# Cross-attention on one core: batch 0's fifth key chunk, the tokens' values and maxima, and the warm-up products

## The chip, the cores and the metric

The kernel runs on one core of one Trainium2 chip. The metric is the device time in microseconds of one execution, the lower the better; runs of the kernel before and after are compared. The engines are named as in the profile: PE (TensorE, matmuls, with PEld for its weight loads), DVE (VectorE), ACT (ScalarE), POOL (GpSimd) and SP (SyncE, which issues most of the DMAs). All data is float32.

## The reference

There are 16 batches of 100 queries, 640 wide, 8 heads of 80. Each batch has 722 context rows of width 384; the last 4 of them are the "tokens", the first 718 the keys.

```python
query = hidden_states @ Wq                      # 100 x 640
keyt, valt = enc @ Wk, enc @ Wv                 # 718 x 640 each
hs = _mha(query, keyt, valt)                    # main attention
ca_q1 = einsum('btc,th->bch', ca, Wq_ca)[:, indices]
ca_hs1 = _mha(ca_q1, residual, residual)        # tokens' first attention (100 x 100)
ca_hs2 = _mha(ca_hs1 @ Wq, ca @ Wk_ca, ca @ Wv_ca)  # tokens' second (100 x 4)
out = (hs + ca_hs2) @ Wout + b_out + residual
```

`_mha` is softmax attention by heads, scaled by 80 ** -0.5.

## The kernel before

The work goes batch by batch, and each batch's iteration also prepares the next ones. In iteration b the kernel makes, for batch b, the scores in three groups (`scores`, L785), the running maximum over the keys (`larger`, L1495; class `Maximum`, L875), the subtraction and exponential of the three score tiles `st` (L1484, L1492), the values (class `Values`, L426) and the attention product `a_ps` (L1741); for batch b + 1 the keys (class `Keys`, L469) and the tokens' first attention (class `Second`, L949); for batch b + 2 the loads.

**Products in forms.** Keys and values are made by a scheme with 15 products of sums ("forms") in place of 18. The sums of the context are made by POOL (`enc_sums`, L497), 13 operations a batch; the sums of the weights once at the start (`weight_sums`, L524), on DVE and POOL. A product is accumulated in a PSUM bank, and after each product the bank is read: copied by ACT the first time a target is written, added by DVE afterwards (`Blocks.go`, L412). So a bank must be read before the next product adds to it. The keys have five chunks of 128 columns; four of them come from `Keys`, the fifth from class `Chunk` (L730): 16 products of 64 columns, two side by side, put between the attention products of the batch before at the places `steps` (L1714 to L1717). For batch 0 itself, the fifth chunk comes from `last_keys` (L720): nine products of 128 columns by 240 keys straight from the raw context, into the two banks of a `pair`, and two ACT copies.

**Tokens.** `Second.products` makes y, DVE takes the part g from it (`take`, L980), POOL multiplies and adds four times for the scores e (`scores1`, L989: L997, L1004), DVE makes their maximum (`softmax1`, L1009) and ACT the exponential (`exponentials1`, L1027). The maximum runs in steps: a transpose, quad, side, mx, spread, a transpose to over, then the subtraction. With `scalar` two spread copies go to ACT, without it one goes to DVE and mx takes four reductions in place of two. The flag `fine` cuts the steps smaller, and `go(n)` lets n of them pass, so the calls with numbers decide where each step stands on its engine. The tokens' values `va` are made once for all batches (L1427 to L1444): six matmuls, an ACT copy, two DMAs to DRAM. Their weights `wvca` stand in one of the two `enc` buffers, into which batch 1's context is loaded later (`load_enc`, L230).

**Kinds of batches.** `PAIRS` names the batches after which two blocks of 128 output rows are projected at once (`project_pair`, L1248); this happens in iterations 3, 6, 8, 11 and 13. `MIXED` are the odd iterations 3 to 13, in which the next pair's queries are made. `PLAIN` (L41) are those without either: 0, 2, 4, 10, 12 and 14.

**Order.** Before the batch loop a planner orders each engine's instructions by their readiness in its model; `tc.issue_after` and `keep_in_program_order` add constraints on one engine. From the loop on (`tc.manual_schedule`, L1462) every engine takes its instructions in the order of the program. The planner may still put early instructions of the loop among the last ones ahead of it. PE, DVE, ACT, POOL and SP's queue each work in order.

PSUM has three pools of two: `pair` (two banks at once), `psumk` and `psum1`; `psum` alternates between the last two. The `wide` tiles of the maxima have two buffers.

Of the kernel before, what the change touches and what calls it, by code (L numbers as in the profile page):

```python
# [40 lines left out]
PLAIN = [b for b in range(B - 1) if b not in (1, *MIXED) and b - 1 not in PAIRS]  # L41
# [101 lines left out]
def kernel(  # L143
# [260 lines left out]
    class Blocks:  # L404
# [7 lines left out]
        def go(self, n=1):  # L412
            for _, (k, (bank, f, to)) in zip(range(n), self.plan):
                first = bank not in self.opened
                if first:
                    self.opened[bank] = self.open(bank)
                at = self.opened[bank]
                self.product(at, f, first, self.ends[bank] == k)
                for out, left in self.places(at, to):
                    if to in self.begun:  # L420
                        self.moved = nc.vector.tensor_tensor(out, left, out, ALU.add)  # L421
                    else:
                        self.moved = nc.scalar.copy(out, left)  # L423
                self.begun.add(to)
# [450 lines left out]
    class Maximum:  # L875
# [12 lines left out]
        def steps(self, top):  # L888
# [24 lines left out]
            if not (self.fine and scalar) or self.fine == "plain":  # L913
                yield
# [34 lines left out]
    class Second:  # L949
# [14 lines left out]
        def products(self):  # L964
# [14 lines left out]
            self.y_v = y_ps[:S, : NH * HG].rearrange("p (h k) -> p h k", h=NH)  # L979
        def take(self, lo, hi):  # L980
            return nc.vector.tensor_copy(self.g[:, lo:hi], self.y_v[:, lo:hi, :T])

        def copy(self):
            self.y = y_sbs[self.b % 2]
            nc.scalar.copy(self.y[:, :, :HT], self.y_v[:, :, T:])
            if self.b > 0:
                self.take(0, NH)
# [21 lines left out]
        def softmax1(self, n=9, hold=False):  # L1009

            if not self.top:
                after = self.b - 1
                self.top = Maximum(
                    e1,
                    f"1_{self.b}",
                    after - 1 in PAIRS or after in PLAIN,
                    "plain" if after in PLAIN else after in MIXED or after - 1 in PAIRS,
                )
# [8 lines left out]
        def exponentials1(self):  # L1027
            nc.scalar.activation(e1[:S], e1[:S], AF.Exp, scale=SCALE)
# [97 lines left out]
    class Last:  # L1126
# [121 lines left out]
        def project_pair(self, between):  # L1248
# [41 lines left out]
            between(2 if self.b + 1 in MIXED else 3)  # L1290
# [4 lines left out]
            read(b4, 1, 0)  # L1295
            product(b2, [(two[:, 4:], last(1))], True)
            read(b2, 1, 1)
            product(b1, [(one[:, 2:4], w(1, 1)), (one[:, 4:], last(1))], False)
            read(b1, 0, 1)
            product(b3, [(two[:, :2], wout2[:, 0])], True)  # L1300
# [33 lines left out]
    for _ in range(5):  # L1334
        nc.tensor.matmul(idle_ps[:, :P], idle, idle, start=True, stop=True)
# [84 lines left out]
    with tc.issue_after(made.ins):  # L1420
        weight_sums(nc.gpsimd, wk4)
    with tc.issue_after(masked.ins):
        keys(load_m(1))
    last_keys(0, enc)
    Keys(0, enc).go(NF)

    va = wide("va")[:, : H // 2]  # L1427
    va_ps = psum("va_ps")
# [11 lines left out]
    for n in range(2):  # L1440
# [3 lines left out]
        )  # L1444
    with tc.issue_after(copied.ins):
# [17 lines left out]
    for b in range(B):  # L1463
# [52 lines left out]
        if b - 1 in PLAIN:  # L1516
            now.exponentials1()
# [12 lines left out]
        if b == 0:  # L1530
# [22 lines left out]
            less = subtract(2)  # L1553
            enc_next = load_rest(b + 2, enc_next)
            keys(m_next)
            now.values2(less)
            enc_sums(enc_next)
        elif b + 1 < B:
# [77 lines left out]
            if last.b in PAIRS:  # L1636
                last.project_pair(second.softmax1)
# [7 lines left out]
            if not mixed and b not in PLAIN:  # L1645
# [54 lines left out]
        if b < B - 1 and not b in MIXED:  # L1700
# [17 lines left out]
        for g in range(2):  # L1718
# [5 lines left out]
            for n, (h, i) in enumerate(order):  # L1724
                if b in PLAIN and (g, n) in ((1, 1), (1, 8), (1, 12)):
                    second.softmax1(1)
                if b < B - 1 and (g, n) in steps:
                    chunk.go()
                    if b not in MIXED and (g, n) == steps[-1]:
# [10 lines left out]
                for lo, hi in QC:  # L1740
# [7 lines left out]
                    )  # L1748
            if b in PLAIN and g == 0:
# [92 lines left out]
```

## Time and profile before

| | |
|---|---|
| three runs | 914.9, 914.14, 911.94 us |
| their median | 914.14 us |
| the profiled execution | 916.26 us |
| its span from first to last instruction | 914.5 us |
| PE busy | 902.7 us (99%) |
| DVE busy | 720.0 us (79%) |
| POOL busy | 706.4 us (77%) |
| ACT busy | 461.9 us (51%) |
| TensorE clock granted | 1.0 |

The profile's times count from the first instruction of the span. In the span the loop's first scores begin at 59.3 us, and those of batch 1 at 101.3 us. A row of a timeline has start, duration (both in us), engine, line of the kernel, operation, the tiles written and read, shapes, how many were merged, and in brackets the idle time before it and what ended it. Each float32 matmul appears as two records.

### The profile page before, as it was taken

How to read it: one execution, taken by the hardware profiler on the slowest of the kernel's cores; microseconds unless marked ns; L12 is line 12 of the kernel's file. 1: busy time of each engine (PE TensorE's matmuls, PEld its weight loads, DVE VectorE, ACT ScalarE, POOL GpSimd, SP SyncE). 2: the span in 40 equal slices, each digit the busy share in tenths (PEclk: the TensorE clock that was granted, in tenths of full speed). 3: DMA queues.
4: the chain of work that ended last, by engine and by line, in shares of the span. 5: the costliest groups of instructions: out<-in, count | busy, mean ns of one | idle time of the engine just before them, and what ended most of it. 6: DMA issues, size and time to landing. Idle time of an engine off the chain costs nothing.

```text
span 914.5 us, 28436 instructions
## 1 busy us (share of the span) xinstructions
PE 902.7 (99%) x12172; PEld 746.1 (82%) x12172; DVE 720.0 (79%) x1288; ACT 461.9 (51%) x907; POOL 706.4 (77%) x684
## 2 busy tenths in 40 slices
PE   9998999999999999999999999999999999999998
PEld 6886879888797878878788787988879888797866
DVE  2659896889848898796987869878895889848983
ACT  2334533747437473653736436364742747437441
POOL 7587999687967879697796968968797687976623
PEclk9999999999999999999999999999999999999999
DMA  8832002031300302131021301203120031310111
GB/s 257 268 96 79 30 32 85 24 106 53 96 18 27 104 24 83 54 86 51 33 75 54 105 32 47 61 25 106 54 81 32 25 106 54 91 37 24 61 46 38
DMA packets 50586, 62.99 MB, mean 69 GB/s; under 512 B 13682, under 2 KB 37810, under 8 KB 50460
## 3 DMA queue, kind: packets, MB, share of 16 engines
q1 hardware_dynamic: 48812, 59.18, 21.1%
q8 instruction: 96, 1.57, 0.7%
q10 hardware_dynamic: 1024, 1.15, 0.4%
q0 software_dynamic: 624, 0.85, 0.3%
q14 instruction: 30, 0.25, 0.1%
HBM read 55.59 MB, written 5.57 MB: 67 GB/s over the span
## 4 chain that ended last, share of the span: by engine, by line
PE 90%; DVE 4%; DMA 3%; SPq 1%; issue 0%; ACT 0%; ACTq 0%; DVEq 0%
PE s_ps L800 12%; PE a_ps L1741 11%; PE v_psA L450 11%; PE v_psB L450 9%; PE k_psA L481 8%; PE k_psB L481 7%; PE o_ps L1265 4%; PE k_psA L761 4%; PE v_psC L450 4%; PE k_psC L481 3%; PE q_ps L618 2%; PE q_ps L560 2%; PE v_psD L450 2%; PE v_psE L450 2%; PE q_psA L618 1%; DMA xT<-in_xt 1%
## 5 line engine op out<-in xcount | busy, mean ns | idle before, releaser
L997 POOL TENSOR_TENSOR e<-ca,g 100x800 f32<-100x800 f32 x64 | 98.0, 1542 | 100.2 <-ACT kT L423 76.2
L1741 PEld LDWEIGHTS a_ps<-vs,st 120*64 120x64 f32 (+3 forms) x3072 | 120.2, 124 | 10.5 <-issue 0.4
L1741 PE MATMUL a_ps<-vs,st 120*64 120x81 f32 (+3 forms) x3072 | 124.2, 233 | 0.0
L516 POOL TENSOR_TENSOR enc<-enc 128x240 f32<-128x240 f32 x144 | 111.7, 786 | 13.8 <-DMA enc<-in_enct 6.8
L1485 DVE TENSOR_TENSOR st<-st,over 120x1600 f32<-120x1600 f32 x48 | 115.2, 2401 | 0.0
L450 PE MATMUL v_psA<-wv_sb,enc 128*120 128x320 f32 x352 | 109.3, 433 | 0.0
L1112 POOL TENSOR_TENSOR hs<-hs,hs 100x640 f32<-100x640 f32 x48 | 94.8, 1975 | 3.8
L481 PE MATMUL k_psA<-enc,wk_sb 128*128 128x240 f32 x384 | 95.4, 371 | 2.1 <-DVE kT L421 1.7
L1105 POOL TENSOR_TENSOR hs<-vb,p 100x640 f32<-100x640 f32 x64 | 89.6, 1411 | 9.1 <-issue 4.8
L1004 POOL TENSOR_TENSOR e<-e,e 100x800 f32<-100x800 f32 x48 | 92.5, 1927 | 3.8
L450 PE MATMUL v_psB<-wv_sb,enc 128*120 128x320 f32 x296 | 91.8, 433 | 0.0
L481 PEld LDWEIGHTS k_psA<-enc,wk_sb 128*128 128x128 f32 x384 | 71.4, 190 | 18.6 <-POOL e L997 2.1
L450 PEld LDWEIGHTS v_psA<-wv_sb,enc 128*120 128x120 f32 x352 | 64.2, 183 | 25.0 <-DVE vs L421 0.5
L1493 ACT ACTIVATE st<-st 120x1600 f32<-120x1600 f32 x48 | 73.9, 1539 | 20.3 <-DVE st L1485 19.6
L1497 DVE TENSOR_TENSOR most<-most,st 120x800 f32<-120x800 f32 x64 | 68.3, 1068 | 14.2 <-ACT st L850 12.9
L481 PE MATMUL k_psB<-enc,wk_sb 128*128 128x240 f32 x320 | 78.0, 366 | 0.3 <-DVE sm L1087 0.3
L800 PE MATMUL s_ps<-qp,kT 64*64 64x100 f32 (+1 forms) x3072 | 73.4, 248 | 0.0
L450 PEld LDWEIGHTS v_psB<-wv_sb,enc 128*120 128x120 f32 x296 | 54.1, 183 | 21.9 <-DVE vs L421 0.4
L800 PEld LDWEIGHTS s_ps<-qp,kT 64*64 64x64 f32 (+1 forms) x3072 | 67.0, 130 | 5.6 <-issue 4.2
L1180 ACT COPY hsT<-turned_hs 32x160 f32<-32x160 f32 (+7 forms) x244 | 67.7, 278 | 3.0
L481 PEld LDWEIGHTS k_psB<-enc,wk_sb 128*128 128x128 f32 x320 | 60.6, 190 | 8.7 <-issue 0.7
L856 ACT COPY st<-s_ps 120x800 f32<-120x800 f32 x64 | 49.8, 830 | 34.3 <-PE s_ps L800 33.6
(209 smaller groups left out, 1904.2 us busy)
## 6 DMA issues: line engine op xcount, KB each, us to landing
vb<-va_d SPq DMA_DIRECT2D x62, 250.0 KB
enc<-in_enct SPq DMA_DIRECT2D x30, 240.0 KB
enc<-in_enct SPq DMA_DIRECT2D x15, 360.0 KB
xT<-in_xt SPq DMA_DIRECT2D x8, 500.0 KB
rest<-in_enct SPq DMA_DIRECT2D x31, 120.0 KB
xn<-in_x SPq DMA_DIRECT2D x11, 320.0 KB
out<-xn SPq DMA_DIRECT2D x11, 320.0 KB
ca<-in_cas SPq DMA_DIRECT2D x16, 156.2 KB
```

The source lines that it names most:

```text
L450: nc.tensor.matmul(at[0][j][:KN, : H // 2], a_form(self.enc, f)[:, j * KN : (j + 1) * KN], wv_there.get(f, wv_sb[:, W_AT[f]]), start=first ...
L481: nc.tensor.matmul(at[:, i * KT : (i + 1) * KT], wk_sb[:, W_AT[f], i], a_form(self.enc, f), start=(first and i == 0), stop=last, skip_grou ...
L516: nc.gpsimd.tensor_tensor(out, left, right, op)
L800: nc.tensor.matmul(s_ps[at][k0:k1, cols], w, rhs, start=not begun & {(at, k) for k in range(k0, k1, 32)}, stop=last, skip_group_check=True,)
L997: first = nc.gpsimd.tensor_tensor(to, self.ca[:, t, :].unsqueeze(1).to_broadcast([S, NH, S]), g[:, :, t].unsqueeze(2).to_broadcast([S, NH, ...
L1004: made = nc.gpsimd.tensor_tensor(e, e, to, ALU.add)
L1105: first = nc.gpsimd.tensor_tensor(to, self.vb[t][:S].rearrange("p (h d) -> p h d", h=NH), p2[:, :, t].unsqueeze(2).to_broadcast([S, NH, D] ...
L1112: nc.gpsimd.tensor_tensor(sums, sums, to, ALU.add)
L1485: return nc.vector.tensor_tensor(st[i], st[i], top.over[:KN].unsqueeze(1).to_broadcast([KN, 2, ROWS]), ALU.subtract,)
L1493: nc.scalar.activation(st[i], st[i], AF.Exp, scale=SCALE)
L1497: most_now = nc.vector.tensor_tensor(most[:KN], most[:KN], st[i][:, u], ALU.max)
L1741: nc.tensor.matmul(a_v[lo:hi, h % 4], st[i // 2][: KEYS[i], i % 2, h * S + lo : h * S + hi], block(i, h // 4)[: KEYS[i], h % 4], start=(i ...
```

## The change

`PLAIN` loses batch 0. Around that:

- **Warm-up.** 21 matmuls of 32 columns by 32 in place of 5 of 128 by 128.
- **Before the loop.** Batch 0's keys are made in two goes, eight products and seven; between them stand the tokens' values `va`, now in a bank of a `pair`. Batch 0's first maximum of the tokens (`softmax1`) moves from the loop's head to behind the last key addition, and the copy of `low` into the score tile's unused rows to behind the tokens' scores in the program.
- **Batch 0's iteration.** Batch 1's fifth key chunk is made by `last_keys` behind batch 0's keys, ahead of the attention, in place of `Chunk` inside it. The exponential of the third score tile comes right behind its subtraction. Batch 1's tokens' maximum runs on DVE alone: four steps behind batch 0's tail work, and the rest with the subtraction and the exponential behind the attention's second half, ahead of that half's normalisation.
- **Iterations 6 and 8.** The maximum's steps inside `project_pair` go 1, 2, 2, 1 in place of 1, 3, and the remaining ones behind it; over is made inside, and the subtraction moves into the attention's second half, at (1, 6).
- **Plain iterations (2, 4, 10, 12, 14).** The empty step ahead of spread is gone, so spread stands at the attention's place (1, 18), ahead of y's copy; the following batch makes the exponential of e in two halves.
- For batch 1, `take` stands ahead of y's copy in the program.

```diff
-PLAIN = [b for b in range(B - 1) if b not in (1, *MIXED) and b - 1 not in PAIRS]
+PLAIN = [b for b in range(2, B - 1) if b not in MIXED and b - 1 not in PAIRS]
...
-            if not (self.fine and scalar) or self.fine == "plain":
+            if not (self.fine and scalar):
                 yield
...
+            if b == 1:
+                self.take(0, NH)
...
-            if self.b > 0:
+            if self.b > 1:
                 self.take(0, NH)
...
-                    "plain" if after in PLAIN else after in MIXED or after - 1 in PAIRS,
+                    after in (*MIXED, *PLAIN) or after - 1 in PAIRS,
...
-        def exponentials1(self):
-            nc.scalar.activation(e1[:S], e1[:S], AF.Exp, scale=SCALE)
+        def exponentials1(self, parts=1):
+            w = ROWS // parts
+            for lo in range(0, ROWS, w):
+                part = e1[:S, lo : lo + w]
+                nc.scalar.activation(part, part, AF.Exp, scale=SCALE)
...
-            between(2 if self.b + 1 in MIXED else 3)
+            between(2)
             product(b4, [(two[:, 2:4], wout2[:, 1])], True)
             product(b1, [(sum1, w(0, 1))], False)
             read(b1, 1, 1)
             product(b4, [(two[:, 4:], last(0))], False)
             read(b4, 1, 0)
+            if self.b + 1 not in MIXED:
+                between(2)
             product(b2, [(two[:, 4:], last(1))], True)
             read(b2, 1, 1)
             product(b1, [(one[:, 2:4], w(1, 1)), (one[:, 4:], last(1))], False)
             read(b1, 0, 1)
+            if self.b + 1 not in MIXED:
+                between(1)
...
-    for _ in range(5):
-        nc.tensor.matmul(idle_ps[:, :P], idle, idle, start=True, stop=True)
+    for _ in range(21):
+        nc.tensor.matmul(
+            idle_ps[:32, :32], idle[:, :32], idle[:, :32], start=True, stop=True
+        )
...
     with tc.issue_after(made.ins):
         weight_sums(nc.gpsimd, wk4)
+        nc.scalar.copy(
+            sts[0].rearrange("p a r -> p (a r)")[96:],
+            low[96:].to_broadcast([P - 96, 2 * ROWS]),
+        )
...
-    Keys(0, enc).go(NF)
-
+    first_keys = Keys(0, enc)
+    first_keys.go(8)
     va = wide("va")[:, : H // 2]
-    va_ps = psum("va_ps")
+    va_ps = bank("va_ps")
+    turn[0] += 1
...
+    first_keys.go(NF)
+    with tc.issue_after(first_keys.added.ins):
+        second.softmax1()
...
-            now.softmax1()
-            nc.scalar.copy(
-                sts[0].rearrange("p a r -> p (a r)")[96:],
-                low[96:].to_broadcast([P - 96, 2 * ROWS]),
-            )
...
         if b - 1 in PLAIN:
-            now.exponentials1()
+            now.exponentials1(2)
...
             less = subtract(2)
+            exponential(2)
+            last_keys(b + 1, enc)
             enc_next = load_rest(b + 2, enc_next)
             keys(m_next)
             now.values2(less)
             enc_sums(enc_next)
+            second.softmax1(4)
...
-                last.project_pair(second.softmax1)
+                last.project_pair(lambda n: second.softmax1(n, True))
...
-            if not mixed and b not in PLAIN:
+            if b == 1:
                 second.softmax1(8)
...
-        if b < B - 1 and not b in MIXED:
+        if 0 < b < B - 1 and b not in MIXED:
             chunk = Chunk(b + 1, enc)
             chunk.go(2)
...
-                if b < B - 1 and (g, n) in steps:
+                if 0 < b < B - 1 and (g, n) in steps:
                     chunk.go()
+                    if b - 1 in PAIRS and b not in MIXED and (g, n) == (1, 6):
+                        second.softmax1()
...
+            if b == 0 and g == 1:
+                second.softmax1()
+                second.exponentials1()
```

More of the change, by code (lines that the diff above doesn't have):

```diff
@@ L420, in go @@
                     if to in self.begun:
-                        self.moved = nc.vector.tensor_tensor(out, left, out, ALU.add)
+                        self.added = nc.vector.tensor_tensor(out, left, out, ALU.add)
                     else:
-                        self.moved = nc.scalar.copy(out, left)
+                        nc.scalar.copy(out, left)
                 self.begun.add(to)
```

## The prediction

> **What bounds the kernel now.** First the page's totals, then the waits of TensorE (PE), since an engine that is busy all the time can only be helped by removing its work or its few gaps.
>
> ```profile
> span 914.5 us, 28436 instructions
> PE 902.7 (99%) x12172; PEld 746.1 (82%) x12172; DVE 720.0 (79%) x1288; ACT 461.9 (51%) x907; POOL 706.4 (77%) x684
> ```
>
> ```profile
> PE k_psA L481 <- DVE kT L421: 1.7, 1, 1.7
> ...
> PE w_ps L1394 <- DMA kT<-in_wkt: 1.1, 1, 1.1
> PE k_psA L761 <- DVE kT L751: 0.9, 2, 0.5
> PE k_psA L761 <- DVE kT L421: 0.9, 1, 0.9
> PE o_ps L1265 <- DVE xn L1276: 0.7, 2, 0.3
> PE m_ps L1370 <- issue: 0.5, 1, 0.5
> PE k_psA L481 <- DVE wk_sb L546: 0.5, 1, 0.5
> PE k_psB L481 <- DVE sm L1087: 0.3, 1, 0.3
> ```
>
> PE is idle for 914.5 - 902.7 = 11.8 us in all. A row gives the wait, what ended it, its sum, how often and the longest. With the 1.1 at the very start (the 1.13 row under Warm-up) they name 7.7 us; most of the rest is the end, when the last output leaves. So the change moves the time only where it touches one of these rows or alters what PE computes. By place: 3.2 us before 38 us (DVE's zeroing, weights that are late), 2.9 us in batch 0 (L421 twice, L1087), 1.6 us in two later batches (L751, L1276). Nothing stands for batches 1, 2, 4, 10, 12 and 14. Every forecast below is a subtraction from these rows, plus the difference in PE work.
>
> **Batches 6 and 8: the tokens' maximum.** These are the two batches that project a pair of row blocks, but make no queries. The timelines of PE and DVE in batch 6 show both waits; batch 8 has the same two (the rows above count two of each, 0.7 and 0.9 in all).
>
> ```profile
> 413.55 1.85 PE L1265 MATMUL o_ps<-wout_sb,hsT 128*128 128x320 f32 x6 [0.34 <-DVE xn L1276]
> ...
> 420.22 0.63 PE L761 MATMUL k_psA<-enc,w_sums 128*64 128x240 f32 x4 [0.45 <-DVE kT L751]
> ```
>
> ```profile
> 410.49 0.98 DVE L893 TENSOR_REDUCE quad<-turned 128x25 f32<-128x800 f32 x1
> 411.50 0.71 DVE L896 TENSOR_REDUCE side<-quad 32x25 f32<-32x25 f32 x4
> 412.24 0.65 DVE L905 TENSOR_REDUCE mx<-side 32x25 f32<-32x100 f32 x2
> 412.92 1.28 DVE L1276 TENSOR_TENSOR xn<-o_ps,xn 128x320 f32<-128x320 f32 x3
> ...
> 417.33 1.00 DVE L926 STREAM_TRANSPOSE over<-spread 128x800 f32<-128x800 f32 x1
> 418.36 1.36 DVE L1023 TENSOR_TENSOR e<-e,over 100x800 f32<-100x800 f32 x1
> ```
>
> PE's 0.34 waits for a bank that DVE reads at 412.92, because three steps of the maximum stand in front. The change lets two steps through there and puts mx behind the next read: the bank's read starts at 412.24, 0.65 earlier, more than 0.34. PE's 0.45 waits for the chunk's first additions, which DVE begins only when over (1.00) and the subtraction (1.36) are done, at 419.7. The change puts over ahead of the pair's last two reads and the subtraction into the second half of the attention, (1, 6). The additions start some 1.4 earlier, the subtraction's time, more than 0.45. What is late next: the two moved reads end about 1.0 later, but free a bank pair that the next scores alone take, some 10 us on; the subtraction runs among the attention's last 3 us, and only e's exponential, which ACT takes after it, needs it. I cost the new waits at nothing. Term: 2 x (0.34 + 0.45) = **-1.6 us**.
>
> **Batch 0's fifth chunk.** Before, 16 products of half width (two column halves side by side) run inside batch 0's attention; after, 9 full ones stand in front of it.
>
> ```profile
> 89.14 0.43 PE L761 MATMUL k_psC<-enc,w_sums 128*64 128x120 f32 x4
> 90.42 0.63 PE L761 MATMUL k_psA<-enc,w_sums 128*64 128x240 f32 x4 [0.85 <-DVE kT L421]
> ...
> 100.45 0.92 PE L970 MATMUL y_ps<-m,xT 128*64 128x72 f32 x20
> ```
>
> From the chain of waits, records of the same form as a full product, and of the attention:
>
> ```profile
> 38.27 0.81 PE k_psB L481 x4
> ...
> 97.68 1.69 PE a_ps L1741 x48
> ```
>
> ```profile
> 92.30 1.53 ACT L1493 ACTIVATE st<-st 120x1600 f32<-120x1600 f32 x1
> ```
>
> A full product of 240 columns is two records of 0.81 / 4 = 0.2025, so nine take 18 x 0.2025 = 3.65. Attention: 1.69 / 48 = 0.0352 a record, 192 of them 6.76. After: 3.65 + 6.76 = 10.41. Before: 89.14 to 100.45 is 11.31, the 0.85 wait in it. What they replace took 11.31 - 0.85 - 6.76 = 3.7, so PE's work stays the same and the wait goes: the full products go into a bank pair that no key product uses, and cover the time in which DVE empties k_psC. Term: **-0.9 us**; if the wait came back in front of them, it would be 0. ACT now makes st's last exponential before their two copies; it ends at 93.8, and the attention needs it at 89.1 + 3.65 and two thirds of its first half (2.25), 95.0. DVE loses seven additions of 0.41.
>
> **What DVE does in that room.**
>
> ```profile
> 90.28 1.81 DVE L1485 TENSOR_TENSOR st<-st,over 120x1600 f32<-120x1600 f32 x1
> ```
>
> Batch 1's maximum is now made by DVE alone (two more mx reductions, its own spread). Its over and subtraction stand ahead of the second half's normalisation, which frees a_ps. The last subtraction of st ends at 92.1. By batch 6's rows the transpose takes 1.0, quad 1.0, side 0.7, four mx 1.3 and spread, as wide as over, 1.0; over 1.0 and the subtraction 1.4 follow, and I add 0.7 for each half's normalisation: 100.9, and 100.0 with the shift of the next part. PE wants those banks in its second scores, near 101. I cost it at 0; the bound is the subtraction held up by two POOL products as long as L997's below, +3.0.
>
> **The tokens' values among the keys.** Rows of PE, SP, POOL and DVE, in this order:
>
> ```profile
> 48.84 1.83 PE L1431 MATMUL va_ps<-wvca,tokens 128*64 128x320 f32 x12
> 78.52 1.05 PE L481 MATMUL k_psA<-enc,wk_sb 128*128 128x240 f32 x4 [1.66 <-DVE kT L421]
> ```
>
> ```profile
> 50.72 1.82 SPq L234 DMA_DIRECT2D enc<-in_enct  x3
> ```
>
> ```profile
> 57.15 0.69 POOL L516 TENSOR_TENSOR enc<-enc 128x240 f32<-128x240 f32 x1 [3.02 <-DMA enc<-in_enct]
> ...
> 70.29 3.04 POOL L997 TENSOR_TENSOR e<-ca,g 100x800 f32<-100x800 f32 x2
> ```
>
> ```profile
> 63.37 1.02 DVE L1514 TENSOR_TENSOR most<-st 128x800 f32<-128x800 f32 x1 [4.68 <-ACT st L856]
> 65.70 2.93 DVE L1497 TENSOR_TENSOR most<-most,st 120x800 f32<-120x800 f32 x2 [1.31 <-ACT st L850]
> ...
> 69.13 0.18 DVE L981 COPY g<-y_ps 100x32 f32<-100x32 f32 x1
> 69.22 4.97 DVE L1497 TENSOR_TENSOR most<-most,st 120x800 f32<-120x800 f32 x2
> ```
>
> Batch 1's context goes into the buffer that the tokens' value weights hold, so its load (50.72) waits for the last va product. Seven of the fifteen key products, 0.81 each, now follow va: it ends 5.7 earlier, and POOL's sums can start up to 3.02 earlier, at 54.1. What follows on POOL shifts with them, but L997 needs g, which DVE makes at 69.13. DVE's maxima are the long pole: one takes 1.02 alone, yet the pair at 65.70 takes 2.93 beside POOL's sums, and the pair at 69.22 takes 4.97, the second one stuck until both L997 are through. PE waits 1.66 at 78.52 for what stands behind. With the sums over by 65, the first pair takes 2.0 and the rest of DVE's row starts 0.9 earlier; the second pair again meets L997, which I leave at 4.97, the row's own value. Term: **-0.9 us**, out of the 1.66. Bounds: -2.5, if it meets one L997 only; +1.0, if each of its two maxima waits in turn, for both L997 (3.0) and for the addition behind them (1.9, as long as L1004's mean on the page): 1.0 + 3.0 + 1.0 + 1.9 = 6.9 in place of 4.97, less the 0.9. The second maximum starts at about 70.2, before L997 at 70.29, and still ends after both: starting first did not give it its turn. The page "SBUF — State Buffer" of the Trainium skill ("Who interferes with whom") has whichever of the two issues first hold the shared port for its whole instruction, which this row doesn't bear out; by it the term would be -2.4, as in the third rival.
>
> The moved va brings its copy and two DMA issues to ACT among the key copies. They have the time of the three products after which a key bank is needed again, 2.4 us, and I cost them at 0; if they are longer, each us is lost once. The first tokens' maximum keeps its place on DVE, behind the last key addition and POOL's scores; batch 0's low copy was already early on ACT. Both 0.
>
> **Warm-up.** 21 small products replace 5; both end about where the first weights land.
>
> ```profile
> 1.13 2.50 PE L1335 MATMUL idle_ps<-idle 128*128 128x128 f32 x10 [1.13 <-DVE idle L1332]
> 3.62 1.42 PE L391 MATMUL v_ps<-wv_sb,rest 128*120 128x320 f32 x2
> ...
> 7.31 0.70 PE L391 MATMUL v_ps<-wv_sb,rest 128*120 128x320 f32 x2
> 7.85 1.24 PE L391 MATMUL v_ps<-wv_sb,enc 128*120 128x320 f32 x4
> ```
>
> Six value records take 3.7 us until 7.31, against 0.27 each after it (two in 7.31 to 7.85); the granted clock stands at 1.00 all the while, so only these durations show the slow start. Up to 2.1 could be won, or as much lost by a later switch, but PE afterwards waits 0.5 (L1370), 1.1 (L1394, a DMA) and 0.5 (L546, behind the wq loads): a gain ends in these waits, and a loss of up to 2.1 is covered by them. Term: 0.
>
> **Plain batches (2, 4, 10, 12, 14).** Spread moves ahead of y's copy on ACT, and the exponential of e is split in halves. PE waits for neither now; the split adds one instruction to ACT, at 51% the idlest engine. Term 0; uncovered, five times at most what the shortest copy in this list costs, 5 x 0.2 = +1.0.
>
> **Sum.** -1.6 - 0.9 - 0.9 = -3.4. The profiled execution took 916.26 (914.5 and 1.8 around it), 2.1 above the median of the three runs; the terms are differences, so I take them from the median: 914.14 - 3.4 = **910.8 us**.
>
> **Rivals.**
> - The load isn't earlier, because SP's queue or PE's order holds it back: SP's queue is served in order, and other loads wait in it; against it, its visible release is va's last product. Third term 0: -2.5, 911.7. Chance 0.18.
> - POOL's scores block each maximum in turn: third term +1.0, -1.5, 912.7. The 4.97 speaks for it; that DVE has its first maximum under way when g is out speaks against. Chance 0.14.
> - The port goes to the first starter: the second pair takes 1.0 + 1.5 + 1.0 = 3.5 in place of 4.97, -4.9 in all, 909.2. The start at 70.2 speaks against it. This is what "SBUF — State Buffer" of the Trainium skill would give. Chance 0.10.
> - A wait takes the removed one's place: a_ps is freed late behind batch 1's subtraction, +3.0 - 3.4 = -0.4, 913.7. Chance 0.08.
> - Slower: PE runs in order, and the tokens' products are put ahead of the keys while wvca is still on its way.
>
> ```profile
> 33.83 0.50 DVE L1405 COPY wq_sb<-st 128x256 f32<-128x256 f32 x2 [0.35 <-DMA st<-in_wq]
> ```
>
> ```profile
> 20.00:40.00 20.00, 17.95 (x144) 15.95 (x141) 12.11 (x40) 6.51 (x12) 10.71 (x20) 1.00 0.84 262
> ```
>
> At 48.84 they never waited. wvca's 960 KB follow wq, whose end releases DVE at 33.8; at 262 GB/s (last column) they land near 37.5, an estimate. The keys now start near 37.2; each us that PE stands after that is lost, and from 37.2 + 3.4 = 40.6 on the kernel is slower. Taken halfway from there to 48.8, at 44.7: +7.5 - 3.4 = +4.1, 918.2. The early estimate speaks against it. Chance 0.08.
>
> **Numbers.** The forecast keeps 0.42. Faster by over 0.3% (2.7 us, about what a measurement of this kernel can tell from no change): 0.42 + 0.10 = 0.52; within it 0.18 + 0.14 + 0.08 = 0.40; slower 0.08. The range, 908.4 to 914.0, takes in all but the last case, with a little at each end for the runs' spread (911.94 to 914.9).
>
> **What would show it.** Right: no PE wait on L1276's and L751's successors in batches 6 and 8; last_keys of batch 1 directly behind the keys; POOL's first sum near 54; the first pair of maxima near 2.0; PE's wait at 78 about half. Wrong: a PE wait for wvca near 37, for a_ps near 100, a second pair over 5 us, or new waits in the plain batches.

## The result and the profile after

| | before | after |
|---|---|---|
| median | 913.96 us (6 runs, 911.94 to 914.9) | 908.75 us (6 runs, 907.88 to 909.39) |
| span of the profiled execution | 914.5 us | 907.1 us |
| PE busy | 902.7 us | 901.1 us |

The ratio is 0.9946, with a 95% interval of 0.9933 to 0.996: 5.2 us faster (3.7 to 6.1 by the interval) where 3.4 were forecast. The spans differ by 7.4 us; the profiled execution of before is one of its longer ones (916.26).

The view of waits of the kernel after, by sum, times and longest (us), has no line left for a wait of batch 0 or of the batches 6 and 8. One is new, `v_psC`, in batch 1:

```profile
PE idle_ps L1344 <- DVE idle L1341: 1.1, 1, 1.1
PE m_ps L1381 <- issue: 0.5, 1, 0.5
PE v_psC L450 <- ACT vs L423: 0.3, 1, 0.3
```

PE starts each batch with its scores, so the start of the first scores (L800) cuts the trace into batches. PE's rows at those places, before, for batches 0, 6 and 7, then after, for batches 0, 1, 6 and 7 (before's row for batch 1, at 101.3, stands in the prediction's working):

```profile
59.26 0.74 PE L800 MATMUL s_ps<-qp,kT 64*64 64x100 f32 x24
...
370.10 0.91 PE L800 MATMUL s_ps<-qp,kT 64*64 64x100 f32 x32
...
427.82 0.65 PE L800 MATMUL s_ps<-qp,kT 64*64 64x100 f32 x20
```

```profile
57.70 1.51 PE L800 MATMUL s_ps<-qp,kT 64*64 64x100 f32 x60
...
96.25 1.60 PE L800 MATMUL s_ps<-qp,kT 64*64 64x100 f32 x64
...
365.74 1.00 PE L800 MATMUL s_ps<-qp,kT 64*64 64x100 f32 x36
...
422.21 1.00 PE L800 MATMUL s_ps<-qp,kT 64*64 64x100 f32 x36
```

Batch 0 takes 101.30 - 59.26 = 42.04 before and 96.25 - 57.70 = 38.55 after; batch 6 takes 57.72 and 56.47. All such differences, from the same rows of every kernel that was run (they differ by up to 0.01 from the rounded rows):

| kernel (all in us) | first scores at | batch 0 | batch 1 | batch 6 | batch 8 | median |
|---|---|---|---|---|---|---|
| before | 59.26 | 42.03 | 56.14 | 57.73 | 57.80 | 913.96 |
| after | 57.70 | 38.55 | 56.95 | 56.48 | 56.48 | 908.75 |
| after_again | 59.41 | 38.55 | 55.86 | 56.64 | 56.48 | 908.9 |
| undo_warm | 59.30 | 38.55 | 55.88 | 57.22 | 56.94 | 910.18 |
| undo_va | 58.03 | 38.55 | 56.63 | 56.48 | 56.48 | 911.7 |
| undo_68 | 58.21 | 38.55 | 56.94 | 57.69 | 57.70 | 911.97 |
| undo_chunk | 59.32 | 43.76 | 56.45 | 56.48 | 56.48 | 914.68 |
| fix_pool | 57.96 | 38.56 | 56.60 | 56.48 | 56.48 | 908.93 |
| seen | 58.10 | 38.55 | 56.41 | 56.48 | 56.48 | 908.57 |
| undo_plain | 58.82 | 38.56 | 56.96 | 56.48 | 56.48 | 909.51 |
| only_chunk | 58.59 | 38.56 | 55.93 | 57.89 | 58.08 | 913.93 |
| only_va | 65.91 | 39.65 | 55.93 | 57.70 | 57.97 | 919.68 |
| only_seen | 57.71 | 39.41 | 55.93 | 58.12 | 57.69 | 912.29 |
| va_seen | 57.21 | 38.55 | 57.62 | 56.48 | 56.48 | 909.58 |

So the profiled executions place the change in four columns: batch 0 (-3.48), batches 6 and 8 (-1.25, -1.32), batch 1 (+0.81) and the start (-1.56), of which the last is spread and not the change, as the runs below show. Batches 9 and 10 are 0.30 and 0.28 shorter too, but undo_68 and the kernels before with one part alone mostly take the same as the kernel after (54.64 and 46.79): this belongs to the one execution of before, not to the change.

What answers in the profile after to the rows of batch 0 shown before: the SP queue's load of batch 1's context, POOL's first sum and first product of the tokens, DVE's two pairs of maxima, PE's products.

```profile
43.43 1.81 SPq L234 DMA_DIRECT2D enc<-in_enct  x3
```

```profile
52.48 0.71 POOL L516 TENSOR_TENSOR enc<-enc 128x240 f32<-128x240 f32 x1
...
66.96 4.41 POOL L999 TENSOR_TENSOR e<-ca,g 100x800 f32<-100x800 f32 x2 [3.47 <-ACT st L856]
```

```profile
64.13 2.02 DVE L1517 TENSOR_TENSOR most<-most,st 120x800 f32<-120x800 f32 x2 [0.90 <-ACT st L850]
...
66.74 3.23 DVE L1517 TENSOR_TENSOR most<-most,st 120x800 f32<-120x800 f32 x2
```

```profile
84.04 0.97 PE L481 MATMUL k_psA<-enc,wk_sb 128*128 128x240 f32 x4
84.85 1.38 PE L702 MATMUL kT_ps<-enc,wk 128*128 128x240 f32 x6
...
88.59 1.62 PE L1761 MATMUL a_ps<-vs,st 120*64 120x81 f32 x40
95.40 0.93 PE L970 MATMUL y_ps<-m,xT 128*36 128x72 f32 x20
```

The load goes out 7.3 us earlier (43.43 against 50.72), 5.7 when counted from the first scores, and the sums no longer wait for a DMA. The first pair of maxima takes 2.02 in place of 2.93, the second 3.23 in place of 4.97. The full products run from 84.85 to 88.59, behind the keys without a gap, and the attention to 95.40: 10.55 us, 10.41 in the prediction. No row of PE in batch 0 carries idle time.

### The profile page after: what moved, and what is told of

Same layout as the page of the kernel before. It is cut to its first block, busy times and chain, and to the rows that moved or that the text cites. A ratio compares the mean times of both kernels' runs of the same rounds, so it can differ in the third digit from the quotient of the medians.

```text
span 907.1 us, 28462 instructions
## 1 busy us (share of the span) xinstructions
PE 901.1 (99%) x12190; PEld 746.1 (82%) x12190; DVE 719.3 (79%) x1283; ACT 459.6 (51%) x906; POOL 704.4 (78%) x684
## 4 chain that ended last, share of the span: by engine, by line
PE 92%; POOL 3%; DVE 2%; DMA 1%; issue 1%; ACT 0%; POOLq 0%; ACTq 0%; DVEq 0%
PE a_ps L1761 11%; PE s_ps L800 11%; PE v_psA L450 10%; PE v_psB L450 9%; PE k_psA L481 8%; PE k_psB L481 6%; PE o_ps L1270 5%; PE k_psA L761 4%; PE v_psC L450 3%; PE k_psC L481 3%; PE q_ps L618 2%; PE q_ps L560 2%; PE v_psD L450 2%; PE v_psE L450 2%; PE q_psA L618 1%; POOL enc L516 1%
## 5 line engine op out<-in xcount | busy, mean ns | idle before, releaser
L1505 DVE TENSOR_TENSOR st<-st,over 120x1600 f32<-120x1600 f32 x48 | 118.0, 2460 | 0.0
L516 POOL TENSOR_TENSOR enc<-enc 128x240 f32<-128x240 f32 x144 | 108.7, 765 | 9.8 <-DMA enc<-in_enct 2.8
L1517 DVE TENSOR_TENSOR most<-most,st 120x800 f32<-120x800 f32 x64 | 65.7, 1026 | 14.5 <-ACT st L850 13.3
L800 PE MATMUL s_ps<-qp,kT 64*64 64x100 f32 (+1 forms) x3072 | 73.7, 248 | 0.0
L800 PEld LDWEIGHTS s_ps<-qp,kT 64*64 64x64 f32 (+1 forms) x3072 | 67.1, 130 | 5.7 <-issue 4.3
```

The lines of the kernel that those rows point to most:

```text
L516: nc.gpsimd.tensor_tensor(out, left, right, op)
L800: nc.tensor.matmul(s_ps[at][k0:k1, cols], w, rhs, start=not begun & {(at, k) for k in range(k0, k1, 32)}, stop=last, skip_group_check=True,)
L1505: return nc.vector.tensor_tensor(st[i], st[i], top.over[:KN].unsqueeze(1).to_broadcast([KN, 2, ROWS]), ALU.subtract,)
```

## The experiments

**The same kernel once more, and the start.** No edit; the question was whether the first scores' 57.70 in place of 59.26 belongs to the change.

> The changed kernel once more, beside the four variants. Theory A (the start's 1.6 us are spread between executions): the first scores begin between 57.5 and 59.5 us, not at 57.7 again of necessity; from the first scores on every batch takes what it took in the first trace, within 0.1 us. Theory B (the start's 1.6 us come from the change): 57.7 within 0.3. The time: 0.9946 of before, within 0.002.

Measured: 908.9 us (4 runs), ratio to before 0.9949 (0.9934 to 0.9964). Its first scores start at 59.41, as before's do, and over the rows of the table it lies from 57.2 to 59.4 (only_va apart), for both kinds of kernel. The start's 1.56 is no gain of the change, as theory A said, though batch 1 doesn't keep its length within 0.1. Batch 1 takes 55.86 here, 56.95 in the other execution of the same code, and batch 2 starts only 0.6 later though batch 0 started 1.7 later: batch 1 gives part of an early start back.

**The warm-up undone.**

```diff
-    for _ in range(21):
-        nc.tensor.matmul(idle_ps[:32, :32], idle[:, :32], idle[:, :32], ...)
+    for _ in range(5):
+        nc.tensor.matmul(idle_ps[:, :P], idle, idle, start=True, stop=True)
```

> The five large warm-up products again, all else as after. Theory A (warm-up ends in later waits for weights): the first weight products become fast within 0.5 us of where they do in the changed kernel, the first scores begin within the spread of the other runs, time as after, ratio to before 0.994 to 0.996. Rival (the small products won the 1.6 us of the start): the first scores begin 1 to 1.6 us later than in the changed kernel run beside it, ratio 0.996 to 0.997.

Measured: 910.18 us, ratio 0.9961 (0.9946 to 0.9975), beside 908.9 of after_again. The ratio lies where the rival had it, but the first scores start at 59.30 against 59.41: the trace gives the start nothing. It is longer in batches 6 and 8 (57.22, 56.94), which this edit doesn't touch; PE's waits there, 0.55 and 0.24 at L1040, are put down to "issue", and no run says where they come from. The two intervals overlap: a difference of about 1 us stays open.

**Batches 6 and 8 undone.**

```diff
-            between(2)
+            between(2 if self.b + 1 in MIXED else 3)
...
-                    if b - 1 in PAIRS and b not in MIXED and (g, n) == (1, 6):
-                        second.softmax1()
```

(and the two later `between`, the flag at `project_pair` and the condition `b == 1`, as in the kernel before)

> Iterations 6 and 8 as before, all else as after. Theory A (a wait of PE costs its listed gap and 0.15 to 0.25 more, the overlap that a restart loses): each of the two takes 1.2 to 1.35 us longer than after, 2.5 us in all, ratio to before 0.9970 to 0.9978. Rival (the listed gap is the cost, as the prediction had it): 0.79 each, 1.6 in all, the rest of the stages' gain coming from elsewhere. If batches 9 and 10 also lose 0.3 each, their gain belongs to these iterations too.

Measured: 911.97 us, ratio 0.9985 (0.9973 to 0.9996), 3.1 above after_again. In its view of waits both pairs are back, as before:

```profile
PE k_psA L761 <- DVE kT L751: 0.8, 2, 0.4
PE o_ps L1270 <- DVE xn L1281: 0.7, 2, 0.3
```

Listed they are 1.5 us; the batches are 57.69 - 56.48 = 1.21 and 57.70 - 56.48 = 1.22 longer, 2.4 together. A wait of PE costs more than its listed gap. The gap is counted from the modelled end of the record before, and records behind one another overlap: the four of the product at 84.04 in the profile after last 0.97 in all, and the next product begins 0.81 later. The 0.16 between is lost on top of the gap when PE stops. The single records of undo_68's batch 6 give the whole of it. The one behind the first wait begins 0.78 after the one before it, where the others stand 0.27 apart: 0.34 of gap and 0.16 of overlap. It also lasts 0.51 in place of 0.43, and the next one begins 0.07 later for that. So a listed 0.34 costs 0.58; the second wait, listed 0.41, gives the other 0.62 of the 1.21. The traces are as theory A said. The ratio is above its 0.9970 to 0.9978: the times put 3.1 between the kernels where the traces put 2.4, and undo_68's ten executions spread over 2.6 (910.49 to 913.1).

**The values' move undone.**

```diff
-    first_keys.go(8)
+    first_keys.go(NF)
-    va_ps = bank("va_ps")
-    turn[0] += 1
+    va_ps = psum("va_ps")
```

> The tokens' values behind all of batch 0's keys again, all else as after. Theory A (the earlier load takes POOL's sums off DVE's maxima, and with the maxima PE's wait): POOL's first sum of batch 1 starts 2 to 3 us later after the first scores, the first pair of maxima takes 2.9 instead of 2.0, the second 4 to 5 instead of 3.2, and PE waits again in batch 0, for 1.5 to 2.5 us with what a restart costs; the batch takes 40.5 to 41 us instead of 38.6; ratio to before about 0.9965. Rival (the full products alone did it): batch 0 stays at 38.6 to 39.

Measured: 911.7 us, ratio 0.9971 (0.9955 to 0.9986). The ten executions lie in two groups: 909.0 to 909.2 (three) and 911.2 to 913.1 (seven). The profiled one is of the first group, and its batch 0 takes 38.55, as with the values early and as the rival said; the median is what theory A said. DVE's pairs and POOL's end of the row:

```profile
64.47 2.55 DVE L1515 TENSOR_TENSOR most<-most,st 120x800 f32<-120x800 f32 x2 [0.93 <-ACT st L850]
...
67.61 2.39 DVE L1515 TENSOR_TENSOR most<-most,st 120x800 f32<-120x800 f32 x2
```

```profile
64.84 4.30 POOL L516 TENSOR_TENSOR enc<-enc 128x240 f32<-128x240 f32 x3
69.09 1.15 POOL L1062 DMA_DIRECT2D vb<-va_d  x2
70.25 3.04 POOL L999 TENSOR_TENSOR e<-ca,g 100x800 f32<-100x800 f32 x2
```

POOL, late with its sums, reaches the tokens' products at 70.25, when the second pair (67.61 to 70.00) is just over. Before, POOL reached them at 70.29, as here, but the pair began at 69.22, 1.6 later than here. So a shift of less than 1.6 us of one row against the other decides whether the two products fall between the two maxima, which is called the meeting below. In the kernel after, the sums are over before DVE's pairs, and one product falls between the maxima of the second pair.

**Batch 1's chunk undone** (16 half-width products inside the attention again).

```diff
-            last_keys(b + 1, enc)
...
-        if 0 < b < B - 1 and b not in MIXED:
+        if b < B - 1 and b not in MIXED:
             chunk = Chunk(b + 1, enc)
```

> The kernel after, with batch 1's fifth key chunk again as 16 products of half width inside batch 0's attention. Theory A: the nine full products do the same work and their gain is the wait alone. Then PE's wait for the chunk's bank, 0.85 in the profile before, is back in batch 0, and the restart around it costs about 1.1, as the spacing there did in the profile before (1.117 between two products that otherwise stand 0.2 apart); the other short chunk wait costs about 0.5. Batch 0 takes 39.6 to 40.2 in place of 38.55, and the time is 1.0 to 1.6 above the kernel after, some 910 to 910.5. Rival B: with the maxima of batch 1 now on DVE behind batch 0's tail, the additions of the chunk queue behind them, so that more than before is lost: batch 0 over 40.5, and 911 or more. Rival C: batch 1, where POOL is the bound when batch 0 is short, gives the later start back: batch 0 longer by 1, batch 1 shorter by up to 0.8, the time within 0.4 of the kernel after.

Measured: 914.68 us, ratio 1.001 (0.9994 to 1.0026): the whole gain of the change is gone, and batch 0, at 43.76, is longer than before the change. PE's waits, and the rows of DVE and ACT that cause the first two of them:

```profile
PE k_psC L761 <- ACT kT L753: 1.9, 1, 1.9
PE k_psA L761 <- DVE kT L751: 1.3, 1, 1.3
PE k_psA L761 <- DVE kT L421: 1.2, 1, 1.2
```

```profile
89.82 1.00 DVE L891 STREAM_TRANSPOSE turned<-e 128x800 f32<-128x800 f32 x1
...
93.98 0.98 DVE L923 COPY spread<-mx 128x800 f32<-128x800 f32 x1
95.00 0.41 DVE L751 TENSOR_TENSOR kT<-k_psA,kT 64x240 f32<-64x240 f32 x1
```

```profile
90.00 1.54 ACT L1513 ACTIVATE st<-st 120x1600 f32<-120x1600 f32 x1 [1.33 <-DVE st L1505]
91.44 0.50 ACT L753 COPY kT<-k_psC 64x120 f32<-64x120 f32 x2
```

The chunk's banks must be read between its products; in the change those readers stand behind batch 1's maximum on DVE (89.82 to 94.96) and behind the score tile's exponential on ACT (90.00 to 91.54), which this edit leaves in its early place. The third wait, 1.2, is the one that the kernel before has as 0.85. The full products need no reading between, so they let maximum and exponential stand there. This is rival B.

**The chunk alone**, in the kernel before.

```diff
             less = subtract(2)
+            exponential(2)
+            last_keys(b + 1, enc)
...
-        if b < B - 1 and not b in MIXED:
+        if 0 < b < B - 1 and not b in MIXED:
```

> The kernel before, with one part of the change alone: batch 1's fifth key chunk as nine full products ahead of batch 0's attention (and the third score tile's exponential ahead of its copies), batch 1's maximum as before. Theory A, the prediction's term: PE's 0.85 wait goes and nothing else; with the restart it is worth 0.9. Batch 0 takes 41.1 in place of 42.03, and the time is 0.9 below the kernel before. Rival B: taking the chunk back out of the kernel after cost 5.8, so the full products are worth most of the change by themselves: 4 or more below. Theory C, to which the traces point: that 5.8 arose because in the kernel after DVE's row stood full of batch 1's maximum, which the full products cover; then the part alone gives only A's 0.9.

Measured: 913.93 us, ratio 0.9997 (0.9981 to 1.0012), which reaches from 1.7 us faster to 1.1 slower. Rival B is out; theory C's 0.9 is inside. By the trace: its batch 0 takes 38.56, in an execution in which the second pair of maxima met no product (2.38); only_seen, below, has the same pair (2.38) and before's chunk, and takes 39.41. The difference of 0.85 is the chunk's wait.

**The values alone**, in the kernel before.

```diff
-    Keys(0, enc).go(NF)
+    first_keys = Keys(0, enc)
+    first_keys.go(8)
-    va_ps = psum("va_ps")
+    va_ps = bank("va_ps")
+    turn[0] += 1
...
+    first_keys.go(NF)
```

> The kernel before, with one part of the change alone: the tokens' values among batch 0's keys. Theory A: POOL's sums end by 64 in place of 69, the first pair of maxima takes 2.0, the second about 3.2 in place of 4.97 (one POOL product between the two), and DVE's row behind them starts 4 earlier, so that PE's waits of 1.66 and 0.34 in batch 0 go: 2.3 with the restarts; and the chunk's 0.85 too if DVE stays ahead: batch 0 takes 38.9 to 39.8, the time is 2.3 to 3.2 below the kernel before. Rival B, the prediction's term: half of the 1.66 goes, 0.9 below. Rival C: the second pair meets both POOL products still, nothing changes but the first pair, and the time is within 0.5.

Measured: 919.68 us, ratio 1.0063 (1.0041 to 1.0085), 5.9 slower. Batch 0 does what theory A said (39.65, without the 1.66 and the 0.34, the chunk's 0.85 grown to 1.27), but its scores start at 65.91. DVE's row and PE's, before the loop:

```profile
49.14 1.01 DVE L891 STREAM_TRANSPOSE turned<-e 128x800 f32<-128x800 f32 x1 [6.75 <-POOL e L1004]
...
51.96 0.31 DVE L905 TENSOR_REDUCE mx<-side 32x25 f32<-32x100 f32 x1
52.19 0.64 DVE L421 TENSOR_TENSOR kT<-k_psC,kT 128x480 f32<-128x480 f32 x1
```

```profile
46.68 0.97 PE L481 MATMUL k_psB<-enc,wk_sb 128*128 128x240 f32 x4
52.88 1.97 PE L481 MATMUL k_psC<-enc,wk_sb 128*128 128x240 f32 x4 [5.23 <-DVE kT L421]
```

PE's granted clock in four stretches of the same trace (span of the stretch, its length, busy us and count of PE, PEld, DVE, ACT and POOL, then the clock):

```profile
47.00:52.80 5.80, 0.66 (x4) 0.27 (x2) 3.51 (x8) 0.00 (x0) 5.72 (x15) 0.90 0.70 197
52.80:56.20 3.40, 3.31 (x8) 2.86 (x9) 3.21 (x8) 0.00 (x0) 3.24 (x6) 0.50 0.00 0
56.20:58.00 1.80, 1.80 (x7) 1.75 (x6) 1.73 (x3) 0.56 (x1) 1.72 (x3) 0.50 0.00 0
58.00:60.00 2.00, 2.00 (x12) 2.00 (x11) 0.90 (x1) 0.33 (x1) 1.92 (x2) 0.88 0.00 0
```

The planner now puts the tokens' first maximum ahead of the last key additions on DVE. There it waits 6.75 for POOL's scores, with the additions behind it, and PE waits 5.23 for them. The clock is at 0.50 in the windows behind the stop, and the 0.88 of the last one puts its return at about 58.5 (half speed for 0.48 of the 2.00); the 0.90 of the first puts its fall at about 51.6, some 4 us into the stop. The next four records take 1.97 in place of 0.97: half of the 5.6 us from 52.88 to 58.5, about 2.8, is lost on top of the wait (an estimate from these rows). "TensorE: Matmul & The Clock Gate" of the Trainium skill (Part 1, on the clock gate) has the clock at half after an idle window of about 3.4 us, until a busy window has passed; the trace agrees with the half and with a wait longer than that. The kernel after has the same order of keys and values, but there `softmax1` is issued after `first_keys.added`, and its first step stands behind the last addition:

```profile
48.54 0.66 DVE L421 TENSOR_TENSOR kT<-k_psC,kT 128x480 f32<-128x480 f32 x1 [0.15 <-PE k_psC L481]
49.21 1.01 DVE L891 STREAM_TRANSPOSE turned<-e 128x800 f32<-128x800 f32 x1
```

So the move of the first maximum, which the prediction had at 0, seems to be what keeps the values' move from costing this. No run takes that constraint alone out of the kernel after.

**POOL's products held back**, in the kernel before: they wait for the second maximum.

```diff
-            second.scores1()
+            second.scores1(seen)
```

> The kernel before, with something that the change doesn't do: POOL's products of the tokens in batch 0 wait for both maxima of DVE. Theory A: the 4.97 of the second pair is the two POOL products between its maxima; then it takes 2.0, DVE's row behind it starts 3.0 earlier, and PE's 1.66 and 0.34 go, 2.3 with the restarts, the 0.85 perhaps as well: 2.3 to 3.2 below the kernel before, like the values' move alone. Rival B: the maxima are slow for another reason (the context's sums, DMA writes), the pair stays above 4, and the time is within 0.5. Rival C: POOL's products, 2.0 later, are late for ACT and for the next maximum, and 1 or more of the gain is lost.

Measured: 912.29 us, ratio 0.9986 (0.9973 to 1.0), 1.5 below before. Batch 0 takes 39.41, without the 1.66 and the 0.34; the chunk's wait stays, listed 0.9. Against before's 42.03 this is 2.62 for two waits listed as 2.0. In this execution the products start right behind POOL's own row, after the pair's end at 69.51, so that the wait itself held nothing back:

```profile
67.13 2.38 DVE L1497 TENSOR_TENSOR most<-most,st 120x800 f32<-120x800 f32 x2
```

```profile
69.77 3.04 POOL L997 TENSOR_TENSOR e<-ca,g 100x800 f32<-100x800 f32 x2
```

What the wait does over many executions is in the times alone. The highest of ten runs is 913.87 here, of 22 runs of before 917.11. This fits theory A's mechanism, but 1.5 is under its 2.3 to 3.2. That not every execution of before has the meeting would explain it; it was not counted.

**Both: values late and products held back**, in the kernel after (the two edits above).

> The kernel after, with two edits: the tokens' values behind all keys again (the time of that alone fell into two groups, around 909.1 and 912.6), and POOL's tokens' products waiting for both maxima. Theory A: the two groups are executions in which the POOL products do and don't come between the two maxima; with the wait they can't, so all executions lie with the lower group, 908.5 to 910, the spread under 2, and batch 0 takes 38.6. Rival B: the second group comes from something else that the late load brings (the sums beside the first pair, the loads' arrival): then there are still executions at 912 to 913.

Measured: 909.58 us, ratio 0.9947 (0.9928 to 0.9966); six runs from 908.38 to 910.26, none in the upper group that undo_va had seven times in ten. This is theory A, by the times: once a product can't fall between the maxima, the upper group is gone. No execution of that group was profiled.

**The products held back in the kernel after**, and **batch 1's subtraction on DVE**:

```diff
-            second.scores1()
+            second.scores1(seen)
```

```diff
-            now.scores2(nc.gpsimd)
+            now.scores2(nc.vector if b == 1 else nc.gpsimd)
```

> The kernel after, with the tokens' products on POOL in batch 0 made to wait for both of DVE's maxima. In the profile after the second pair of maxima takes 3.23, one of the two behind one POOL product. Theory A: the two engines take turns, and the pair takes 2.0 without POOL beside it; PE isn't waiting for DVE in batch 0 any more, so batch 0 stays at 38.5, and POOL's products end about 1 later. Theory B: POOL's row is the bound of batch 1, so what POOL loses comes back there: batch 1 longer by 0.5 to 1, and the time 0.5 to 1 above the kernel after when the start is early. Rival: POOL has 1 us of room until batch 1: the time is within 0.3 of the kernel after.

> The kernel after, with one instruction moved: batch 1's subtraction for the tokens' second attention runs on DVE in place of POOL. Theory: batch 1 took 56.95 in place of 55.86 in the execution in which batch 0 began early, because POOL's row is the bound there: ACT's exponential waits for POOL's subtraction, and PE for ACT's copies (listed 0.3 and 0.5). With the subtraction on DVE both waits go, batch 1 takes 55.9 to 56.2 whenever batch 0 begins, and the time is 0.5 to 0.9 below the kernel after, some 908. Rival: POOL's other work of batch 1 (the sums of batch 2's context, the tokens' products) is what is late; then batch 1 still takes 56.5 or more, and the time is within 0.3 of the kernel after. Second rival: DVE, 79% busy, has no room in batch 1, and a PE wait for DVE takes the place: 0.5 or more above.

Measured: 908.57 us (seen), ratio 0.9937 (0.9923 to 0.9951), and 908.93 us (fix_pool), ratio 0.9942 (0.9929 to 0.9956): neither differs from the kernel after (0.9946), and fix_pool's theory, 0.5 to 0.9 below it, failed. In seen the second pair does take its time alone:

```profile
67.15 2.01 DVE L1517 TENSOR_TENSOR most<-most,st 120x800 f32<-120x800 f32 x2
```

and batch 0 stays at 38.55: the 3.23 in the kernel after cost PE nothing. Theory B of seen failed as stated: the products start 2.4 later (69.39 against 66.96), but that goes into POOL's idle time ahead of its row at 88 us (2.29 there in seen, 4.79 in the kernel after), and batch 1 doesn't get longer (56.41). What batch 1 waits for is later on POOL's row. POOL's subtraction and ACT's exponential of the kernel after:

```profile
121.79 0.24 POOL L1081 TENSOR_TENSOR e<-s,mx 100x32 f32<-100x32 f32 x1
```

```profile
122.07 0.23 ACT L1087 ACTIVATE e<-e 100x32 f32<-100x32 f32 x1 [9.12 <-POOL e L1081]
122.20 0.73 ACT L423 COPY vs<-v_psC 120x320 f32<-120x320 f32 x2
```

PE's new wait (0.3 at 122.66) is for that copy. From this subtraction to batch 2's scores it is 31.4 us in after, undo_plain and seen, though batch 0 began at 57.70, 58.82 and 58.10: that fits POOL's row setting batch 1's end, though seen lists no wait of PE in batch 1. In after_again (122.24, no wait of PE either) it is 31.6. fix_pool, which takes the subtraction off POOL, has no such wait, but one of 0.2 for DVE in batch 1, and its batch 1 takes 56.60: the numbers of its first rival, and no version that is faster.

**The plain batches undone.**

```diff
-            if not (self.fine and scalar):
+            if not (self.fine and scalar) or self.fine == "plain":
                 yield
...
-            now.exponentials1(2)
+            now.exponentials1()
```

> The kernel after, with the plain batches 2, 4, 10, 12 and 14 as before: an empty step ahead of spread, and e's exponential in one piece in the batch that follows. Theory, as predicted: nothing, since PE waits for neither; batches 2 to 5 and 10 to 15 keep their lengths within 0.1, and the time is within 0.3 of the kernel after. Rival: the split and the earlier spread gave the mixed batches 3, 5, 11 and 13 the 0.06 each and batch 10 the 0.28 by which they were shorter in the profile after: then 0.5 above the kernel after.

Measured: 909.51 us, ratio 0.9941 (0.9925 to 0.9958). The mixed batches 3, 5, 11 and 13 are each 0.06 longer than after, as they were before. That is 0.24 in all, the rival's first half, and less than the times can tell. Its second half is not shown: batch 10 takes 46.96 here, but 46.79 or 46.80 in only_chunk, only_va and only_seen, which keep the plain batches as before too.

## Why the prediction was right, point by point

- **Direction and range** held: 908.75 in 908.4 to 914.0, faster by 5.2. The forecast of 3.4 was too small in two terms.
- **Batches 6 and 8, -1.6: mis-sized.** The mechanism was right (no waits, no new ones), and undo_68 gives 2.4 for 1.6. The step that failed was "every forecast below is a subtraction from these rows": the listed gap leaves out what PE loses in stopping.
- **Batch 0's fifth chunk, -0.9: right by the traces**, 0.85 between only_chunk and only_seen; only_chunk's time (0.9981 to 1.0012) can't tell it from nothing. That PE's work stays equal was right too (10.55). What the part-by-part sum didn't see is that the parts hang together: without the full products, with the maximum on DVE and the early exponential on ACT, batch 0 is 5.2 us longer (undo_chunk).
- **The tokens' values, -0.9: right mechanism, wrong size.** The load was earlier and the first pair took 2.0, as forecast. But "the second pair again meets L997, which I leave at 4.97" failed: it took 3.23, and all of the 1.66 and the 0.34 went, not half. Against the meeting of the traced execution of before this is worth 2.62 (42.03 - 39.41), near the bound of -2.5; against an execution without it, the traces give the move nothing (38.55 in after and in undo_va). The times say that the kernel before mixes them; in after, after_again, seen, fix_pool and undo_plain all times lie from 907.9 to 910.7.
- **The third rival** (second pair 3.5, 909.2 us) is what happened to the pair in the kernel after, and its time is nearest. The nearness of the time is in part luck: its 2.4 for the values is more than the 1.5 to 1.7 found below, and its 1.6 for batches 6 and 8 less than the 2.4. DVE's first maximum there and POOL's first product, each by itself:

```profile
66.74 0.98 DVE L1517 TENSOR_TENSOR most<-most,st 120x800 f32<-120x800 f32 x1
```

```profile
66.96 2.16 POOL L999 TENSOR_TENSOR e<-ca,g 100x800 f32<-100x800 f32 x1 [3.47 <-ACT st L856]
```

  The maximum started first and takes its 0.98; the product takes 2.16, where it takes 1.54 alone. Then the second maximum waits for one product, not for two. "SBUF — State Buffer" of the Trainium skill ("Who interferes with whom") calls the shared port an exclusive lock and has the issue order decide who blocks, and this trace agrees. The trace of before doesn't: there the second maximum, begun at about 70.2, ahead of the products' 70.29, waited through both, 3.0 us.
- **DVE's room, 0: right.** The normalisations stand at 93.48 and 96.12, the subtraction ends at 96.0, and PE's scores at 96.25 carry no wait.
- **ACT's copies and DMA issues, 0, and the slower case** (values ahead of their weights): right, the values at 41.55 don't wait.
- **The first maximum, 0**: right for the kernel after, where its place costs nothing; in only_va, which has the values' move without it, the time is 5.9 above before.
- **Warm-up and plain batches, 0**: within what could be told. The traces give 0 and 0.24.
- **Batch 1** was forecast at nothing and gives 0 to 0.8 of an early start back on POOL's row; why its length ranges from 55.86 to 57.62 over all runs is not settled in full (in va_seen a PE wait of 0.7 for a chunk addition comes to it).

The account by the traces: 2.4 to 2.6 in batches 6 and 8, 0.85 for the chunk and 0.24 in the mixed batches make 3.5 to 3.7. The rest of the measured 5.2, 1.5 to 1.7, is put down to the values' 2.62 in that share of executions that had the meeting, less what batch 1 gives back; only_seen puts the first of these at 1.5 by itself. Both are loose: the 5.2 can be 3.7 to 6.1, only_seen's 1.5 can be 0 to 2.5, and the share was not counted in traces.

## What to carry to other kernels

An engine at 99% gains from a removed wait more than the wait's listed gap (here 2.4 for 1.6), so measure the stage from start to start. When two engines' rows run free beside each other, one profiled execution shows one meeting of them: look at the spread of the times before putting a price on it, and prefer the order that takes the meeting away. Undoing the full products cost 5.2 in their batch, and making them alone gave 0.85: a part may be worth most as the cover for another. A part that is priced at nothing (here the place of one maximum) may be what keeps another from losing.

## What the runs showed of the hardware

- Two DVE maxima of 0.98 each take 2.01 alone (seen), 2.4 beside POOL's sums (undo_va, only_seen), 3.23 when they take turns with POOL's products (after), 4.97 when the second waits through two of them (before).
- A stop of PE of 5.23 us brought its granted clock to 0.50 from some 4 us into the stop until some 5.6 us of work behind it (only_va); the waits of 0.3 to 1.9 in the other runs did not.
- POOL loses too: three sums take 2.15 in after (60.25), ahead of DVE's pairs, and 4.30 beside them in undo_va (64.84).
- PE lost 0.58 for a listed gap of 0.34, and 0.62 for one of 0.41 (undo_68).
